# Squares from SBUF, other kept pieces and a rearranged tail in the normalisation stage of a four-layer image kernel

## The chip, the cores and the metric

The kernel runs on one core of one Trainium2 chip, as one launch. The metric is the device time of that launch in microseconds (us). The core has a matrix engine (TensorE, PE in the profile; PEld is its weight load), a vector engine (VectorE, DVE), an activation engine (ScalarE, ACT), a general engine (GpSimd, POOL) and a synchronising engine (SyncE, SP) that mostly issues transfers. Matrix products land in PSUM[...]; everything else lies in SBUF (128 partitions) or in DRAM.

## What is computed

The input `x` is an image of 256 x 256 pixels with 128 channels, float32. Four layers follow each other; each normalises its input over groups of four channels and adds its result to it. Only the first layer's beginning is touched by the change:

```python
# layer 0: attention over each image row, 4 heads of 32 channels
z   = _gn(x)                                   # group normalisation over the whole image
mu  = mean(z, axis=-1);  var = mean((z - mu)**2, axis=-1)
zn  = (z - mu) * rsqrt(var + 1e-5) * ln_scale + ln_bias
q, k, v, g = zn @ Wq, zn @ Wk, zn @ Wv, sigmoid(zn @ Wg)
bias = zn @ Wb                                 # one number per pixel and head
a = softmax(q k^T / sqrt(32) + bias)           # per image row and head; the bias is shared by all rows
x = x + (g * (a v)) @ Wo
```

The later layers (a gated recurrence of 16 steps, a triangle product and a 3 x 3 convolution) come after it and are the same in both kernels.

## The kernel before

The image has 65,536 pixels; they are worked in 32 pieces of 2048 pixels (1 MiB each), numbered m = 0 to 31.

**Statistics pass** (`statistics`, line 206). All 32 pieces are read once, for the mean and variance of each channel. Eight of them stay in SBUF (`kept`, line 360): pieces 0, 4, 8, ..., 28. The pass reads the other pieces first, the kept ones last. At its end `group_affine` and `centering` make a matrix `lc` and a column `cb`, so that `lc` times a piece, plus `cb`, is the group-normalised piece with its channel mean already taken away.

**Normalisation stage** (`attention`, lines 376 to 503), where the change lies. Pieces that were not kept are read again, three ahead, through SP's queue (`load`, buffers `xin`, three of them). A piece goes through these steps:

- `turn(m)`: sixteen 128 x 128 transposes on TensorE into two PSUM tiles `pt`, copied to `xo` (channels on partitions) by ACT (first half) and DVE (second half). Then the next piece's `load`, and POOL's queue stores `xo` to DRAM (`xT`), except for the last three pieces.
- `centre(m)`: for each half b, `zc = lc x xo` on TensorE, into a PSUM tile of 1024 columns. Then ACT squares `zc + cb` into `sq`, and DVE adds `cb` to `zc` and writes `zn`. Both read the same PSUM tile.
- `variance(m)`: TensorE takes the mean of the squares over the channels (`var`, four parts side by side on 32 partitions each); ACT makes `rs = exp(-0.5 ln(var + eps))`.
- `normalise(m)`: TensorE spreads `rs` over the partitions (`pr`, four products of 32 rows each, two per half, two instructions each); DVE multiplies `zn` by it, half by half; POOL applies `ln_scale` and `ln_bias` and its queue stores `zn` to DRAM (`znT`), except for the last three pieces.
- `pair_bias(m)`: TensorE makes the bias of the piece's pixels (`pbias`), DVE copies it (`bi`), and four small stores of 8 KB put it into DRAM (`biasD`) through SP's queue.

The order is written out by hand: nearly all instructions of this stage are pinned to program order on their engine (`mm`, `act`, `tt`, `ts`, `copy`, `transpose`, `acopy`); only transfers, and POOL's scaling, are placed by the framework's planner. The loop of one pass m is

```python
variance(m); centre(m + 1); normalise(m); pair_bias(m - 1); turn(m + 2)
```

The PSUM tiles of `zc`, `pr` and `pt` share one pool of three buffers ("w"[...]), taken in turn; `var`, `pbias` and the projections' `pp...` share a pool of two ("r"). A product can start only when all readers of the tile that last used its buffer are done.

**The tail.** The last three pieces stay in SBUF for the attention loop. Before it starts, `project(n, names)` makes q, k, v and g of the first three row pairs (n = 0, 1, 2) from piece 29: one product each, and a copy by ACT (g through an exponential). `project(0, ...)` stands in the last pass between `centre` and `normalise`; the others after the loop. `load_bias(r0, r1)` brings rows of the bias back from DRAM; the last 16 rows need the bias stores of pieces 30 and 31. After them TensorE transposes the bias (`pbt`, line 745), DVE copies it (`bT`), and the attention loop can add it to its first scores.

The printed code below has `attention`, with all these steps, at the line numbers of the profile.

Of the kernel before, what the change touches and what calls it, by code (L numbers as in the profile page):

```python
# [9 lines left out]
F32 = mybir.dt.float32  # L10
AF = mybir.ActivationFunctionType
# [6 lines left out]
P = 128  # L18
# [3 lines left out]
NH, HD = 4, 32  # L22
# [9 lines left out]
class Kernel:  # L32
# [21 lines left out]
    def act(self, out, in_, func, bias=0.0, scale=1.0, **kw):  # L54
        return self.nc.scalar.activation(out, in_, func, bias=bias, scale=scale, **kw)  # L55
# [4 lines left out]
    def mm(self, out, lhsT, rhs, start=True, stop=True):  # L60
        return self.nc.tensor.matmul(out, lhsT, rhs, start=start, stop=stop)  # L61
# [286 lines left out]
    def attention(self, wp, later, xT, x1T, znT, biasD, HD_, stats1, shift1):  # L348
        nc, tc, I = self.nc, self.tc, self.i
        V = nc.vector  # L350
        x = I["x"].rearrange("b h w c -> (b h w) c")
        NM = NPIX // 2048
        src = lambda m: x[m * 2048:(m + 1) * 2048].rearrange("(b p t) c -> p b (t c)", b=2, t=8)
        with ExitStack() as c:

            bias = wp.tile([P, 2, NH, N], F32, name="bias")
            c1 = c.enter_context(ExitStack())
            kp = c1.enter_context(self.pool(name="kp", bufs=1))

            kept = {m: kp.tile([P, 2, 1024], F32, name=f"kept{m}") for m in range(0, 32, 4)}  # L360
            mv, (w, (lns, lnb), wo, small) = self.statistics(wp, self.attention_weights(wp), HD_, kept, src)
            with self.pool(name="awq", bufs=2, space=PSUM) as ps0:
                ab, mg, _ = self.group_affine(wp, ps0, None, self.g4, "0", True, mv=mv)
                V.tensor_scalar_mul(shift1, mg, -1.0)
                lc, cb = self.centering(wp, ps0, ab, "0")

            def load_bias(r0, r1):
                rows = biasD.rearrange("h (j k) -> j h k", k=N)
                while r0 < r1:
                    t = min(r1, (r0 // P + 1) * P)  # L370
                    nc.sync.dma_start(bias[r0 % P:r0 % P + t - r0, r0 // P], rows[r0:t])
                    r0 = t
# [16 lines left out]
            mm, act, tt, ts, copy = pin(self.mm), pin(self.act), pin(V.tensor_tensor), pin(V.tensor_scalar_add), pin(V.tensor_copy)  # L389
            transpose, acopy = pin(nc.tensor.transpose), pin(nc.scalar.copy)  # L390
            xin, xo, zn, sq, rs = dict(kept), {}, {}, {}, {}
# [11 lines left out]
            def turn(m):  # L403
                if m >= NM:
                    return
                xo[m] = zp.tile([P, 2, P, 8], F32, name="xo")
                for b in range(2):
                    pt = wide("pt").rearrange("c (t p) -> c t p", t=8)
                    for t in range(8):
                        transpose(pt[:, t], xin[m][:, b, t * P:(t + 1) * P], self.ident)  # L410
                    (copy if b else acopy)(xo[m][:, b], pt.rearrange("c t p -> c p t"))
                if m not in kept:
                    load()
                if m < NM - HELD:
                    nc.gpsimd.dma_start(xT[:, m * 2048:(m + 1) * 2048], xo[m].rearrange("c b p t -> c (b p t)"))

            def centre(m):
                if m >= NM:
                    return
                zn[m] = yp.tile([P, 2048], F32, name="zn")  # L420
                for b in range(2):
                    zc = wide("zc")
                    for k in range(2):
                        mm(zc[:, k * 512:(k + 1) * 512], lc, xo[m][:, b].rearrange("c p t -> c (p t)")[:, k * 512:(k + 1) * 512])
                    sq[m, b] = work.tile([P, 1024], F32, name="sq")
                    act(sq[m, b], zc, AF.Square, bias=cb)
                    ts(zn[m][:, b * 1024:(b + 1) * 1024], zc, cb)

            def variance(m):
                var = row("var")  # L430
                for k in range(4):
                    mm(var[32 * k:32 * k + 32], m32, sq[m, k // 2][:, (k % 2) * 512:(k % 2 + 1) * 512])
                rs[m] = work.tile([P, 512], F32, name="rs")
                act(rs[m], var, AF.Ln, bias=self.eps)
                act(rs[m], rs[m], AF.Exp, scale=-0.5)

            def normalise(m):
                pr = [wide("pr") for _ in range(2)]
                for k in range(4):
                    mm(pr[k // 2][:, (k % 2) * 512:(k % 2 + 1) * 512], spread[32 * k:32 * k + 32], rs[m][32 * k:32 * k + 32])  # L440
                for b in range(2):
                    z = zn[m][:, b * 1024:(b + 1) * 1024]
                    tt(z, z, pr[b], ALU.mult)
                    nc.gpsimd.tensor_scalar(z, z, lns, lnb, ALU.mult, ALU.add)
                if m < NM - HELD:
                    nc.gpsimd.dma_start(znT[:, m * 2048:(m + 1) * 2048], zn[m])

            def pair_bias(m):
                if m < 0:
                    return  # L450
                pb = row("pbias")
                for k in range(4):
                    mm(pb[32 * k:32 * k + 32], w["32"], zn[m][:, k * 512:(k + 1) * 512])
                bi = io.tile([P, 512], F32, name="bi")
                copy(bi, pb)
                for k in range(4):
                    s = m * 2048 + k * 512
                    nc.sync.dma_start(biasD[:, s:s + 512], bi[32 * k:32 * k + NH])

            tc.keep_in_program_order(self.table(LN_EXP))  # L460
            for _ in range(3):
# [1 line left out]
            turn(0)  # L463
            turn(1)
            centre(0)
            early = {}

            def project(n, names):
                if n not in early:
                    early[n] = qp.tile([P, 4, 512], F32, name="proj", tag="xin")  # L470
                z = zn[NM - HELD][:, n * 512:(n + 1) * 512]
                for nm in names:
                    pp, o = row("pp" + nm), early[n][:, "qkvg".index(nm)]
                    if nm == "v":
                        for ch in range(4):
                            mm(pp[:, ch * P:(ch + 1) * P], z[:, ch * P:(ch + 1) * P], w["v"])
                    else:
                        mm(pp, w[nm], z)
                    if nm == "g":
                        act(o, pp, AF.Exp, scale=-1.0)  # L480
                    else:
                        act(o, pp, AF.Identity)

            for m in range(NM):
                variance(m)
                centre(m + 1)
                if m == NM - 1:
                    project(0, "qkvg")
                normalise(m)
                pair_bias(m - 1)  # L490
                turn(m + 2)
                if m == 5:
                    self.later_weights(later)
                elif m == 12:
                    self.first_rows = self.row_transforms(later.tile([P, 2, HC], F32, name="hs0"), HD_, 0)
                elif m == NM - 4:
                    load_bias(0, 192)
                elif m == NM - 1:
                    load_bias(192, 240)
            project(1, "qkvg")  # L500
            pair_bias(NM - 1)
            load_bias(240, 256)
            project(2, "qkvg")
            c1.close()
            held = {m: (zn[m], xo[m].rearrange("c b p t -> c (b p t)")) for m in range(NM - HELD, NM)}
# [1135 lines left out]
```

## Time and profile before

| | us |
|---|---|
| median of 3 runs | 4903.11 (4900.88 to 4903.68) |
| the profiled execution: time | 4899.83 |
| the profiled execution: span | 4897.9 |
| TensorE busy | 4716.3 (96%) |
| VectorE busy | 3631.1 (74%) |
| ScalarE busy | 3334.3 (68%) |
| GpSimd busy | 1855.8 (38%) |
| normalisation stage, first `turn` to the bias transposes | 131.8 to 462.0 |

In a row of the timeline, the first two numbers are the start and the length in us; then come the engine, the line of the code that issued it (a helper's line for most: 61 is `mm`, 55 is `act`, 388 is the pinning lambda), the operation, output <- inputs, and the tile shapes. In brackets stands how long the engine had been idle just before, and what ended that. In a row of the chain, there are the start, the length, engine, tile and count. A matrix product in float32 is two instructions, so "x8" means four products. Columns of the windows are explained where they are shown. The PE clock is the share of full speed that TensorE was granted.

### The profile page before, as it was taken

How to read it: one execution, taken by the hardware profiler on the slowest of the kernel's cores; microseconds unless marked ns; L12 is line 12 of the kernel's file. 1: busy time of each engine (PE TensorE's matmuls, PEld its weight loads, DVE VectorE, ACT ScalarE, POOL GpSimd, SP SyncE). 2: the span in 40 equal slices, each digit the busy share in tenths (PEclk: the TensorE clock that was granted, in tenths of full speed). 3: DMA queues.
4: the chain of work that ended last, by engine and by line, in shares of the span. 5: the costliest groups of instructions: out<-in, count | busy, mean ns of one | idle time of the engine just before them, and what ended most of it. 6: DMA issues, size and time to landing. Idle time of an engine off the chain costs nothing.

```text
span 4897.9 us, 78226 instructions
## 1 busy us (share of the span) xinstructions
PE 4716.3 (96%) x30415; PEld 2682.4 (55%) x30415; DVE 3631.1 (74%) x4551; ACT 3334.3 (68%) x5009; POOL 1855.8 (38%) x1290
## 2 busy tenths in 40 slices
PE   8999999999999899999999997999999999999999
PEld 2444555555555433333333332269999943369999
DVE  6666777777777699999999996763533357789886
ACT  6445888888888799999999995543333367762110
POOL 0233555555555466666666664421011000000000
PEclk9999999999999999999999998999999999999999
DMA  8784122222222245555555555986766688854432
GB/s 299 278 315 161 42 85 80 86 83 87 83 87 83 77 101 132 131 132 132 136 131 131 133 132 133 333 328 226 280 243 225 223 336 323 328 206 166 141 123 70
DMA packets 221057, 835.13 MB, mean 171 GB/s; under 512 B 59046, under 2 KB 62396, under 8 KB 172148
## 3 DMA queue, kind: packets, MB, share of 16 engines
q1 hardware_dynamic: 144638, 498.23, 29.7%
q0 software_dynamic: 74752, 331.47, 23.3%
q8 instruction: 244, 4.00, 0.3%
q14 instruction: 127, 1.04, 0.1%
q10 hardware_dynamic: 1296, 0.40, 0.0%
HBM read 497.84 MB, written 265.03 MB: 156 GB/s over the span
## 4 chain that ended last, share of the span: by engine, by line
PE 66%; ACT 14%; DVE 11%; issue 5%; DMA 2%; POOL 1%; SPq 1%; ACTq 0%; DVEq 0%; POOLq 0%
PE z L61 9%; PE m L61 8%; PE zc L61 7%; PE nd L61 7%; PE sc L61 6%; PE po L61 5%; PE ppq L61 3%; PE ppv L61 3%; PE pe L61 2%; PE px L61 2%; PE ppk L61 2%; PE ppg L61 2%; PE py L61 2%; PE pr L61 2%; ACT L946 2%
## 5 line engine op out<-in xcount | busy, mean ns | idle before, releaser
L605 DVE TENSOR_TENSOR e<-sc,bT 128x1024 f32<-128x1024 f32 x512 | 613.7, 1220 | 254.8 <-PE sc L61 254.8
L605 POOL TENSOR_TENSOR ks<-e 128x1024 f32<-128x1024 f32 x256 | 602.1, 2371 | 445.5 <-PE nd L61 428.4
L55 ACT ACTIVATE e<-e 128x1024 f32<-128x1024 f32 x512 | 539.4, 1054 | 41.2 <-DVE e L605 31.5
L1132 DVE TENSOR_TENSOR LR<-z,sg 128x512 f32<-128x512 f32 x256 | 268.5, 1049 | 363.0 <-ACT sg L55 363.0
L61 PE MATMUL m<-U,v 128*128 128x128 f32 x4608 | 514.8, 275 | 0.0
L61 PEld LDWEIGHTS m<-U,v 128*128 128x128 f32 x4608 | 514.6, 192 | 0.0
L61 PE MATMUL z<-wf,zt 128*128 128x128 f32 x4096 | 459.6, 276 | 1.4 <-DVE zn L1132 1.4
L61 PEld LDWEIGHTS z<-wf,zt 128*128 128x128 f32 x4096 | 459.4, 193 | 2.4 <-DVE zn L1132 2.2
L55 ACT ACTIVATE sg<-z 128x512 f32<-128x512 f32 x256 | 152.8, 597 | 307.8 <-PE z L61 307.8
L1264 POOL DMA_DIRECT2D prodD<-o x128 | 69.0, 540 | 617.4 <-ACT o L55 607.5
L61 PE MATMUL sc<-proj 32*128 32x256 f32 x4096 | 299.8, 403 | 3.2 <-DVE e L605 2.4
L974 POOL TENSOR_TENSOR fs<-f 128x512 f32<-128x512 f32 x64 | 177.0, 2766 | 279.3 <-DVE f L971 258.7
L61 PEld LDWEIGHTS sc<-proj 32*128 32x128 f32 x4096 | 188.1, 185 | 160.7 <-PE px L61 94.8
L61 PE MATMUL nd<-e,proj 128*32 128x256 f32 x4096 | 272.8, 384 | 2.6 <-DVE og L605 2.6
L55 ACT ACTIVATE dn<-dn 128x512 f32<-128x512 f32 x384 | 238.0, 620 | 11.1 <-DVE dn L605 7.0
L974 POOL TENSOR_TENSOR u<-t,tr 128x512 f32<-128x512 f32 x64 | 229.7, 3589 | 9.8 <-DVE tr L977 8.4
L974 POOL TENSOR_TENSOR t<-t,v 128x1024 f32<-128x1024 f32 x64 | 209.5, 3274 | 53.5 <-DVE t L971 53.5
L61 PE MATMUL po<-LR 128*128 128x256 f32 x1024 | 222.1, 379 | 6.9 <-DVE LR L1132 6.9
L1517 ACT COPY m4s<-m 128x512 f32<-128x512 f32 x32 | 18.6, 583 | 287.3 <-PE m L61 287.3
L61 PEld LDWEIGHTS po<-LR 128*128 128x128 f32 x1024 | 194.3, 190 | 33.9 <-DVE LR L1132 7.7
L1527 POOL DMA_DIRECT2D out_dram<-ys x32 | 37.0, 1155 | 423.9 <-DVE ys L1525 423.9
L61 PE MATMUL av<-y,ident 128*128 128x512 f32 x384 | 192.4, 610 | 4.0 <-DVE y L971 4.0
(380 smaller groups left out, 10696.7 us busy)
## 6 DMA issues: line engine op xcount, KB each, us to landing
zt<-znT SPq DMA_DIRECT2D x128, 1024.0 KB
xin<-x2T SPq DMA_DIRECT2D x64, 1024.0 KB
znT<-zn POOLq DMA_DIRECT2D x61, 1024.0 KB, 5.2
xin<-in_x_dram SPq DMA_DIRECT2D x48, 1024.0 KB
xr<-x3T SPq DMA_DIRECT2D x46, 768.0 KB
x1T<-x POOLq DMA_DIRECT2D x64, 512.0 KB, 4.9
xf<-x1T SPq DMA_DIRECT2D x64, 512.0 KB
xc<-x1T SPq DMA_DIRECT2D x128, 256.0 KB
```

What stands on the lines that cost most here:

```text
L55: return self.nc.scalar.activation(out, in_, func, bias=bias, scale=scale, **kw)
L61: return self.nc.tensor.matmul(out, lhsT, rhs, start=start, stop=stop)
L605: pin = lambda f: lambda *a, **k: tc.keep_in_program_order(f(*a, **k))
L946: pin(nc.scalar.preload_act_table_set(want))
L974: pin(nc.gpsimd.tensor_tensor(out, a, b_, op))
L1132: pin = lambda f: lambda *a, **k: tc.keep_in_program_order(f(*a, **k))
L1264: nc.gpsimd.dma_start(prodD[g * CQ + d].rearrange("(p a j) -> p a j", p=P, a=2), o.rearrange("p a j b -> p a (j b)"))
L1517: nc.scalar.copy(m4, m[4])
L1527: nc.gpsimd.dma_start(out[row:row + 8].rearrange("r p t c -> p (r t) c"), ys.rearrange("p g k t c -> p (g k t) c"))
```

## The change

Four edits, all in `attention`:

1. In `centre`, DVE's add comes first and writes `zn`; ACT then squares the half from `zn` in SBUF, without a bias, in place of `zc + cb` from PSUM.
2. The kept pieces are 0, 1, 2, 7, 12, 17, 22 and 26 in place of every fourth.
3. The four bias stores of each of the last two pieces alternate between SP's and POOL's queue.
4. Of `project(0)`, only q and k stay ahead of the last `normalise`; v and g come after the loop. Of `project(1)`, only q stays ahead of the last `pair_bias` and `load_bias`; k, v and g come after them.

```diff
-            kept = {m: kp.tile([P, 2, 1024], F32, name=f"kept{m}") for m in range(0, 32, 4)}
+            kept = {m: kp.tile([P, 2, 1024], F32, name=f"kept{m}") for m in (0, 1, 2, 7, 12, 17, 22, 26)}
...
                     sq[m, b] = work.tile([P, 1024], F32, name="sq")
-                    act(sq[m, b], zc, AF.Square, bias=cb)
-                    ts(zn[m][:, b * 1024:(b + 1) * 1024], zc, cb)
+                    z = zn[m][:, b * 1024:(b + 1) * 1024]
+                    ts(z, zc, cb)
+                    act(sq[m, b], z, AF.Square)
...
                 for k in range(4):
                     s = m * 2048 + k * 512
-                    nc.sync.dma_start(biasD[:, s:s + 512], bi[32 * k:32 * k + NH])
+                    q = (nc.sync, nc.gpsimd)[k % 2] if m >= NM - 2 else nc.sync
+                    q.dma_start(biasD[:, s:s + 512], bi[32 * k:32 * k + NH])
...
                 centre(m + 1)
                 if m == NM - 1:
-                    project(0, "qkvg")
+                    project(0, "qk")
                 normalise(m)
...
-            project(1, "qkvg")
+            project(0, "vg")
+            project(1, "q")
             pair_bias(NM - 1)
             load_bias(240, 256)
+            project(1, "kvg")
             project(2, "qkvg")
             c1.close()
```

## The prediction

> **What bounds the kernel now.** I read the page first: TensorE is busy 96% of the span. The change touches one stage, between the statistics pass (ends near 126 us) and the attention loop (from about 462 us), so I went there with the chain that ended last, windows and the timeline. The chain, cut to two passes of the loop over m:
>
> ```profile
> 306.54 1.00 PE pbias L61 x8
> 307.53 1.90 PE pt L388 x16
> 309.43 1.00 PE var L61 x8
> 310.42 3.63 PE zc L61 x8
> 314.05 1.99 PE pr L61 x8
> 316.05 1.00 PE pbias L61 x8
> ```
>
> One pass takes 9.51 us (314.05 less 304.54), and only TensorE is on the chain. The window says the same, and what else is loaded (columns: start:end, length, busy of PE, PEld, DVE, ACT, POOL, PE clock, DMA share, GB/s):
>
> ```profile
> 200.00:300.00 100.00, 100.00 (x516) 43.28 (x520) 70.11 (x65) 47.66 (x52) 36.09 (x42) 1.00 0.85 312
> 326.30:335.80 9.50, 9.50 (x52) 4.08 (x48) 6.55 (x7) 4.57 (x5) 3.49 (x4) 1.00 0.94 385
> 136.00:140.00 4.00, 0.15 (x1) 0.18 (x2) 0.00 (x0) 0.00 (x0) 0.21 (x1) 0.51 0.90 310
> ```
>
> But busy is not working at its peak. `pr` is eight matmuls on 32 rows each: 1.99 us here, 1.07 us (446.86 to 447.93) in the last pass. The timeline says why:
>
> ```profile
> 302.86 1.11 ACT L55 ACTIVATE sq<-zc,cb 128x1024 f32<-128x1024 f32 x1 [0.54 <-PE zc L61]
> 304.07 1.28 DVE L388 TENSOR_SCALAR zn<-zc,cb 128x1024 f32<-128x1024 f32 x1 [2.58 <-issue]
> 304.47 0.30 PEld L61 LDWEIGHTS pr<-rs,spread 32*128 32x128 f32 x4 [0.76 <-ACT sq L55]
> 305.41 0.30 PEld L61 LDWEIGHTS pr<-rs,spread 32*128 32x128 f32 x4 [0.64 <-DVE zn L388]
> ...
> 446.86 1.14 PE L61 MATMUL pr<-rs,spread 32*128 32x512 f32 x8
> ```
>
> The square of the first half reads `zc` from 302.86 to 303.97, the add reads the same buffer from 304.07 to 305.35, and at 305.41 the second four weight loads of `pr` start: they need that buffer (three PSUM buffers serve zc, zc, pr, pr, pt, pt in turn). In the last pass the buffers are long free and the eight run together. DVE had been idle 2.58 us before 304.07.
>
> Two places at the ends:
>
> ```profile
> 139.85 3.44 PE L388 MATMUL pt<-ident,xin 128*128 128x128 f32 x16 [6.05 <-DMA xin<-in_x_dram]
> 443.10 1.12 PE L61 MATMUL ppq<-zn,wq 128*128 128x512 f32 x2 [1.54 <-DVE bi L388]
> 451.04 1.12 PE L61 MATMUL ppk<-zn,rawk 128*128 128x512 f32 x2 [0.99 <-DVE bi L388]
> 460.26 1.75 PE L745 MATMUL pbt<-ident,bias 128*128 128x128 f32 x14 [1.31 <-DMA bias<-biasD]
> ```
>
> **What the Trainium skill says.** *PSUM — Partial Sum Buffer*, "PSUM bank collisions raise a hardware error": two engines on one bank and quadrant must be kept apart, reads against reads included. The trace agrees: every add starts 0.03 to 0.10 us after its square ends. *TensorEngine Tiling (Array Packing)*, "Key Properties": different tiles can load weights and multiply in parallel; here 1.07 against 1.99 us. *TensorE: Matmul & The Clock Gate*, "Part 1: The HAM clock gate": an idle TensorE is put to half clock and needs some 3.4 us of work to return. Here 0.51 at 136 to 140 us, and those transposes take 3.2 us where the ones before took 1.9.
>
> **Part 1: add first, square from SBUF.** Removed: the square's read of `zc`. The add (1.28 us) now starts when `zc` is ready, the square after it. A square from SBUF is 1.054 us in the statistics pass (`sqx`), 1.113 here: 0.06 x 64, on ACT, idle half the time, so worth nothing. Following one pass on the old clock:
> - add b0: 302.9 to 304.2, before `pr` begins (304.47). So all eight `pr` run together: 304.47 to 305.54.
> - `pbias` to 306.54; `pt` needs the buffer of `zc` b1: add b1 304.55 to 305.85, free. Its second half needs `pr` b0: multiply 305.85 to 307.02, transposes there at 307.5. `pt` ends 308.44.
> - square b0 304.3 to 305.35, b1 305.9 to 306.95; `var` needs both at 308.44: 1.5 us spare. `var` to 309.43.
> - DVE: second multiply to 308.2, `bi` copy to 308.9, `xo` copy to 310.1; wanted by `zc` b1 at 311.2. ACT's `xo` copy 307.7 to 308.7, wanted at 309.43.
> Nothing else is late, so the pass becomes, of the chain's rows, 1.00+1.90+1.00+3.63+1.07 = 8.60 us, 0.92 less. DVE (6.55 us), ACT (4.57) and POOL (3.49) still fit.
>
> The transfers have to follow. Two of 1.049 MB are stored per pass and one loaded in four passes of five: 14.7 MB in 43.0 us, 341 GB/s. Before: 11.5 MB in 38.0, 303; the window of 100 us shows 312 at a share of 0.85, so 367 GB/s at full share, and single windows have 385. It fits, at about 0.93. A load has three passes of lead, a store two to three; `xT` lands in 9.9 us (median). Cost taken: nothing; bound: 0 to +0.4 us a pass.
>
> **Part 2: pieces 0, 1, 2 kept.** Piece 1's second load, issued at 134.43, held TensorE from 133.8 to 139.85 and put its clock down. Now `pt(1)` follows at 133.8 and ends at 135.75; `zc(0)` starts there in place of 143.13: 7.4 us. Part 1 gives some back: `var(0)` now waits for add and square in series. zc(0) ends 139.4, add b1 139.5 to 140.8, square to 141.9, `var` to 142.9 against 148.91. `zc(1)` to 146.55, add b1 to 148.0, which frees `pt(2)`: 148.05 against 155.14. **Gain 7.1 us.** The first new wait could be for piece 3: its load goes out at 134.4, and it is transposed at about 157. The bytes of all passes are the same as before.
>
> **Loop.** From `pt(2)` to `pt(31)` there are 29 passes, `pr` in each: 29 x 0.92 = **26.7 us**. The `zc` of piece 31 then ends near 404, against 437.65.
>
> **Part 3: the tail.** From the end of zc(31) to the last transposes of the bias, before: 437.65 to 460.26 = 22.6 us. After, as offsets:
> - `pr` 1.07, `pbias(29)` 2.07. `var(31)` waits for its second square (2.45): ends 3.5.
> - `ppq(0)` needs the buffer of `pbias(29)`: DVE does add, two multiplies, copy until 4.4. `ppq`, `ppk` end 6.3, `pr(31)` 7.35, `pbias(30)` 8.35, `ppv` 9.3.
> - `ppg(0)` needs the buffer of `pbias(30)`, whose copy waits behind the multiplies of piece 31 (7.5 to 9.85) until 10.55: a new stall of about 1.3 us. `ppg` ends 11.5, `ppq(1)` 12.4.
> - `pbias(31)` 12.5 to 13.5 (POOL finished piece 31 at 11.1); then seven projections of 0.93 cover its way to DRAM and back, to 20.0.
> - That way: copy to 14.35, then as before from 455.73 to 460.26, 4.5 us: 18.9. With two of four stores on POOL's queue it is between 0.7 shorter (two SP issues of 0.35 less) and 0.7 longer: *DMA: Bandwidth & Descriptors*, "Anatomy of one DMA", puts the fixed cost of a POOL-issued transfer at about 2 us, no such small one is in the trace. Either is inside 20.0. Were that cover gone it would cost up to 0.7. POOL has nothing else due: the next fold is at 467.9 us before.
> The transposes, now all 16, start at 20.0; two of them (0.24) had been done early. So **2.3 us**, 0.9 of it the `pr` of pass 30.
>
> **Sum.** 7.1 + 26.7 + 2.3 = 36.1 us. Span 4897.9 to 4861.8; the profiled execution took 4899.83, 1.93 more than its span, so 4863.7. The median is 3.28 above that: 4903.11 - 36.1 = **4867 us**. The attention loop and all later stages keep their code; I take them as shifted. Its first matmuls run at half clock (0.50 from 468 to 476 us) after the tail's waits; fewer waits may spare some of this, or not: 0 to -4 us, or +2 where the clock's windows fall worse elsewhere.
>
> **Rivals.**
> - *The transfers become the bound.* For: 0.93 needed, four heavy passes in a row (366 GB/s), windows of a pass before show shares of 0.91 at only 328. Against: three passes of lead, and 429 GB/s from 148 to 152 us. At 326 GB/s a pass takes 9.0 us: 29 x 0.4 = 12 back, 4879.
> - *The release is early but `pr` stays at two and two* (multiplies or a semaphore hold the second pair). For: in the loop it has never been seen together. Against: the 1.07 in the last pass. Then only the ends: 7.1 + 1.4, 4895.
> - *A wait in place of the one removed, slower.* The square now stands behind the add, and `var` behind both. If it came over 1.5 us later than worked out, `var` would hold TensorE; to lose 9.8 us in all, with 8.5 from the ends, a pass must grow by 0.63, so the second square must be 1.5 + 0.92 + 0.63 = 3.0 us late. Only `multiply` x2 ahead of the second add would do that, and the order is written out. From there about 4915.
> - *The planner orders unpinned transfers otherwise*, a load behind bias stores: a pass or two held, +3 to +10: inside the range, and counted in the forecast's own.
>
> **How the numbers follow.** As forecast 0.72 (own range 4861 to 4876); transfers 0.13; no overlap 0.09; slower 0.04; elsewhere 0.02. A measurement can tell about 0.2%, 9.8 us. The range 4860 to 4885 leaves out the last three cases (0.15) and some 0.04 of the first, where the clock spares more than 4 us. Faster: the first two and two thirds of the third, 0.91; same: its other third and "elsewhere", 0.05; slower 0.04.
>
> **What would show it.** `pr` x8 at about 1.07 in every pass; passes of 8.6 us; adds starting before squares, idle before `pr` on DVE's add gone; no wait for `xin` at 139 and clock 1.00 there; no wait of `pbt` for `bias`, a wait of `ppg` for `bi` of 1.3 us. Wrong if `pt` waits for `xin` in the loop, `zc` for `xo`, `var` for `sq`, or if the attention loop's own passes change.

## The result and the profile after

| | before, us | after, us |
|---|---|---|
| median of 4 runs | 4902.92 (4900.88 to 4903.68) | 4862.09 (4859.07 to 4863.21) |
| profiled execution: time | 4899.83 | 4863.21 |
| profiled execution: span | 4897.9 | 4861.1 |

The ratio is 0.9916, with a 95% interval of 0.9899 to 0.9934: 41 us less, between 32 and 50. (A fourth run of the kernel before has joined the three of the table above.) The profiled executions are 36.6 us apart; the forecast was 36.1, which with its 4867 lies inside that interval. The medians are 4 us further apart than the profiled pair. Of the kernel before, the profiled execution was faster than all four runs of the table; of the kernel after, it was the slowest of the four. What the traces explain below is the 36.6 us of this pair.

The chain that ended last, of the changed kernel, over two passes of the loop (start, length, engine, tile, count):

```profile
302.91 1.07 PE pr L61 x8
303.98 1.00 PE pbias L61 x8
304.97 1.90 PE pt L388 x16
306.87 0.99 PE var L61 x8
307.87 3.63 PE zc L61 x8
311.50 1.07 PE pr L61 x8
```

The pass is 8.59 us (311.50 less 302.91). Four of its five parts have the lengths they had; `pr` alone went from 1.99 to 1.07. The timeline of the same pass shows the new order of the two readers (it has `pr` 0.07 us earlier than the chain):

```profile
301.29 1.28 DVE L388 TENSOR_SCALAR zn<-zc,cb 128x1024 f32<-128x1024 f32 x1 [1.66 <-issue]
302.61 1.06 ACT L55 ACTIVATE sq<-zn 128x1024 f32<-128x1024 f32 x1 [1.91 <-DVE zn L388]
302.84 0.31 PEld L61 LDWEIGHTS pr<-rs,spread 32*128 32x128 f32 x8 [0.76 <-issue]
302.84 1.14 PE L61 MATMUL pr<-rs,spread 32*128 32x512 f32 x8
304.27 1.06 ACT L55 ACTIVATE sq<-zn 128x1024 f32<-128x1024 f32 x1 [0.60 <-DVE zn L388]
306.80 0.16 PEld L61 LDWEIGHTS var<-sq,mean 128*32 128x32 f32 x8 [0.17 <-issue]
```

The add is done at 302.57, before `pr` begins at 302.84, so all eight weight loads stand in one row and none waits for DVE. The second square ends at 305.33; `var` starts at 306.80 and had 1.47 us to spare.

The windows (start:end, length, busy of PE, PEld, DVE, ACT, POOL, PE clock, DMA share, GB/s):

```profile
136.00:140.00 4.00, 3.77 (x20) 2.39 (x19) 2.48 (x3) 1.08 (x2) 1.12 (x2) 1.00 0.62 197
200.00:300.00 100.00, 100.00 (x570) 44.33 (x567) 77.27 (x71) 52.23 (x59) 41.16 (x47) 1.00 0.91 338
```

TensorE's clock is at 1.00 where it had fallen to 0.51, and the transfers run at 338 GB/s and a share of 0.91.

The two ends, in the timeline:

```profile
133.89 3.68 PE L388 MATMUL pt<-ident,kept 128*128 128x128 f32 x32 [0.30 <-issue]
...
416.39 1.13 PE L61 MATMUL ppg<-zn,rawg 128*128 128x512 f32 x2 [1.03 <-DVE bi L388]
...
425.70 1.91 PE L749 MATMUL pbt<-ident,bias 128*128 128x128 f32 x16
```

The first two pieces are transposed in one go. The transposes of the bias follow the last projection with no wait; in its place `ppg(0)` waits for the copy `bi`.

To compare kernels whose statistics pass ended at different times, I use one distance from here on, "the stage": from the first `pt` to the first copy `bT`. Before it was 131.86 to 461.18, 329.3 us; after, 133.89 to 426.77, 292.9 us: 36.4 us less, all of the difference of the spans but 0.4. The 0.4 is what two larger differences leave, both outside the change: the first `pt` is 2.0 us later in the run after, and what follows `bT` 2.4 us shorter.

### The profile page after: what moved, and what is told of

It is laid out like the page before. It is cut to its first block, busy times and chain, and to the rows that moved or that the text cites. A ratio compares the mean times of both kernels' runs of the same rounds, so it can differ in the third digit from the quotient of the medians.

```text
span 4861.1 us, 78233 instructions
## 1 busy us (share of the span) xinstructions
PE 4680.3 (96%) x30415; PEld 2669.2 (55%) x30415; DVE 3632.2 (75%) x4551; ACT 3331.2 (69%) x5009; POOL 1858.4 (38%) x1294
## 4 chain that ended last, share of the span: by engine, by line
PE 66%; ACT 14%; DVE 11%; issue 6%; DMA 2%; POOL 1%; SPq 0%; ACTq 0%; DVEq 0%; POOLq 0%
PE z L61 9%; PE m L61 8%; PE zc L61 7%; PE nd L61 7%; PE sc L61 6%; PE po L61 5%; PE ppq L61 3%; PE ppv L61 3%; PE pe L61 2%; PE ppg L61 2%; PE ppk L61 2%; PE px L61 2%; PE py L61 2%; PE var L61 2%; ACT L950 2%
```

## Experiments

### Each part alone

**The first edit alone.**

```diff
-                    act(sq[m, b], zc, AF.Square, bias=cb)
-                    ts(zn[m][:, b * 1024:(b + 1) * 1024], zc, cb)
+                    z = zn[m][:, b * 1024:(b + 1) * 1024]
+                    ts(z, zc, cb)
+                    act(sq[m, b], z, AF.Square)
```

> The kernel before with only the first edit: DVE adds first, ACT squares the half from SBUF. My theory (the early release of the zc buffer lets all eight pr instructions run together): a pass of 8.60 us in place of 9.51, pr at 1.07 in place of 1.99; 29 passes give 26.7 us, the last pr 0.9, the start neither gives nor takes more than 0.3 us. In all 27 to 28.5 us less: about 4875. If pr did not run together in the loop: a pass of 9.5 us and 4900 to 4903.

Measured: 4875.15 us, ratio 0.9942 (0.9925 to 0.9958); the stage 302.0 us, 27.3 less. Its chain:

```profile
308.29 1.07 PE pr L61 x8
309.36 1.00 PE pbias L61 x8
310.35 1.90 PE pt L388 x16
312.25 0.99 PE var L61 x8
313.25 3.63 PE zc L61 x8
316.88 1.07 PE pr L61 x8
```

The pass of 8.59 us is there with this edit alone. The edit does not touch the tail, and the bias transposes still wait (1.76 us at 433.29).

**The second edit alone.**

```diff
-            kept = {m: kp.tile([P, 2, 1024], F32, name=f"kept{m}") for m in range(0, 32, 4)}
+            kept = {m: kp.tile([P, 2, 1024], F32, name=f"kept{m}") for m in (0, 1, 2, 7, 12, 17, 22, 26)}
```

> The kernel before with only the second edit, the kept pieces 0, 1, 2, 7, 12, 17, 22, 26. My theory: the wait of the second piece's transposes for xin (6.05 us) and their half clock go, 7.4 us less, about 4895.5, with passes of 9.51 us as before. Rival, the transfers are hidden anyway or the stall only moves to piece 3: no change, 4902 to 4904, and a wait for xin of several us at piece 3.

Measured: 4898.1 us, ratio 0.9989 (0.9982 to 0.9996), that is 2 to 9 us less; the stage 322.0 us, 7.3 less. `pt(0)` and `pt(1)` stand in one row:

```profile
133.66 3.68 PE L388 MATMUL pt<-ident,kept 128*128 128x128 f32 x32 [0.30 <-issue]
```

The clock from 134 to 138 us is 1.00, and the pass is 9.51 us as before. In its list of waits from 125 to 200 us nothing waits for `xin`: the stall went, it did not move to piece 3.

**The third and fourth edits alone** (stores of the last two pieces on two queues, projections rearranged).

> The kernel before with only the third and fourth edits (bias stores of the last two pieces on two queues; v, g of project(0) and k, v, g of project(1) later). My theory: the bias transposes no longer wait for the bias (1.31 us), ppg(0) waits about 1 us for bi instead; 1.4 us less from the end of zc(31) to the first bT copy (23.5 us before), which the times can hardly tell: 4901 to 4902.5. Rival, the stores on the other queue land later and the wait stays: 4903 to 4904.

Measured: ratio 0.9998 (0.9989 to 1.0007), which tells nothing; the trace does: the stage is 327.3 us, 2.0 less. Its timeline:

```profile
443.04 1.12 PE L61 MATMUL ppq<-zn,wq 128*128 128x512 f32 x2 [1.54 <-DVE bi L388]
...
449.13 1.12 PE L61 MATMUL ppg<-zn,rawg 128*128 128x512 f32 x2 [0.96 <-DVE bi L388]
...
458.44 1.91 PE L748 MATMUL pbt<-ident,bias 128*128 128x128 f32 x16
```

The wait of `pbt` is gone, and so is that of `ppk(1)` (0.99 before); `ppg(0)` waits 0.96. From the end of `zc(31)` to the first `bT` it takes 21.9 us, 1.6 less than before, against 1.4 expected. The other 0.4 of the 2.0 lie at the start of the stage, which these edits do not touch: the wait for `xin` was 5.56 us in this run and 6.05 before.

The three stages add up: 27.3 + 7.3 + 2.0 = 36.6, and the whole change has 36.4. So the parts neither help nor hinder one another by more than some tenths, and a difference of less than half a microsecond between two stages can't be put down to an edit from one trace of each.

### Is it the last reader, or the earlier add?

The order of the two readers turned round, but the square still reads PSUM:

```diff
-                    act(sq[m, b], zc, AF.Square, bias=cb)
-                    ts(zn[m][:, b * 1024:(b + 1) * 1024], zc, cb)
+                    z = zn[m][:, b * 1024:(b + 1) * 1024]
+                    ts(z, zc, cb)
+                    act(sq[m, b], zc, AF.Square, bias=cb)
```

> The kernel before with the order of the two readers turned round but the square still reading zc from PSUM with its bias: DVE adds first, ACT squares zc + cb after it. My theory (what counts is when the last reader of the PSUM buffer is done): the buffer of half 0 is free at the same time as before, pr stays at two and two, a pass of 9.4 to 9.6 us, 4900 to 4906. Rival, that DVE simply starts earlier is what helps, or the multiply behind it: a pass near 8.6 us and 4875.

Measured: 4903.09 us, ratio 1.0000 (0.9991 to 1.0008); the stage 329.5 us. Its timeline:

```profile
306.49 1.28 DVE L388 TENSOR_SCALAR zn<-zc,cb 128x1024 f32<-128x1024 f32 x1 [1.69 <-PE zc L61]
307.81 1.11 ACT L55 ACTIVATE sq<-zc,cb 128x1024 f32<-128x1024 f32 x1 [1.92 <-DVE zn L388]
308.04 0.30 PEld L61 LDWEIGHTS pr<-rs,spread 32*128 32x128 f32 x4 [0.76 <-issue]
308.97 0.30 PEld L61 LDWEIGHTS pr<-rs,spread 32*128 32x128 f32 x4 [0.64 <-ACT sq L55]
```

DVE adds as early as in the changed kernel, and nothing is gained: the second four loads of `pr` wait for the square, until 308.92, in place of the add. So the gain of the first edit is the release of the PSUM buffer by its last reader, and the square's new source is what makes the release early.

### How near the transfers are

**Every piece read again.** Pieces 7, 12, 17, 22 and 26 are kept in the statistics pass but read again in the stage:

```diff
-            xin, xo, zn, sq, rs = dict(kept), {}, {}, {}, {}
+            xin, xo, zn, sq, rs = {m: kept[m] for m in (0, 1, 2)}, {}, {}, {}, {}
...
-            again = [m for m in range(NM) if m not in kept]
+            again = list(range(3, NM))
...
-                if m not in kept:
+                if m > 2:
                     load()
```

> The changed kernel, but pieces 7, 12, 17, 22 and 26, though kept in the statistics pass, are read again like the others: three transfers of 1.049 MB in every pass, 366 GB/s at 8.59 us. Theory: TensorE bounds the pass and the transfers only follow; the changed kernel moved 338 GB/s at a share of 0.91, so 371 at full share, and this just fits: a pass of 8.6 to 8.7 us, 4862 to 4866. Rival (the transfers are already the bound of the changed kernel, or within a hair): a pass of 9.0 us or more and 4874 or more, with waits for xin or for the store of xo.

**A fourth transfer a pass.**

```diff
                     nc.gpsimd.dma_start(xT[:, m * 2048:(m + 1) * 2048], xo[m].rearrange("c b p t -> c (b p t)"))
+                    nc.gpsimd.dma_start(x1T[:, m * 2048:(m + 1) * 2048], xo[m].rearrange("c b p t -> c (b p t)"))
```

> The changed kernel with a fourth transfer in each pass, a second store of xo into a buffer of DRAM that is overwritten later: 19 MiB in five passes, 463 GB/s at 8.59 us, more than can be moved. It measures where the transfers take over. Theory, a ceiling of 371 GB/s: a pass of 10.7 us, about 55 us more in 26 passes, 4917. If the ceiling is the 429 GB/s of the best window: 9.3 us and 4880. If transfers cost nothing whatever their number: 4862.

Measured, with all read again: 4859.45 us, ratio 0.9917 (0.9901 to 0.9934), the stage 292.9 us, the same. With the fourth transfer: 4912.7 us, ratio 1.0021 (1.0011 to 1.0031), the stage 340.2 us, 47.4 more than in the changed kernel. One window of each, first all read again, then the fourth transfer:

```profile
300.00:380.00 80.00, 80.00 (x451) 34.66 (x449) 61.34 (x57) 41.78 (x47) 31.36 (x36) 1.00 1.01 380
```

```profile
200.00:300.00 100.00, 93.20 (x461) 41.15 (x458) 62.71 (x58) 41.89 (x48) 38.46 (x47) 0.93 0.98 397
```

With three transfers a pass TensorE is still busy all the time; with four it is not, and its clock falls too. Now DVE's add waits for the store that still reads its `zn` buffer; from the list of waits:

```profile
DVE zn L388 <- DMA znT<-zn: 51.0, 12, 5.8
```

(us in total, times, the longest.) Over one stretch for all, 160 to 380 us, the changed kernel moved 345 GB/s, the one with all read again 372 at no cost, and the one with the fourth transfer 395, held back by its stores. So the limit for such transfers lies above 372 and, over a long stretch, at about 395; the changed kernel is 13% under that. The fourth transfer goes through POOL's queue like the other stores; whether this queue or all transfers together set the limit, no run tells apart, though the share of 0.98 speaks for the latter. Pieces 7, 12, 17, 22 and 26 need not be kept for the time of this stage; that pieces 0, 1 and 2 are kept is worth the 7.3 us of the second edit.

### How much room the square has

Every square of the changed kernel made two and three times over:

```diff
-                    act(sq[m, b], z, AF.Square)
+                    for _ in range(2):
+                        act(sq[m, b], z, AF.Square)
```

(This is the first of two kernels; the second has range(3).)

> The changed kernel with every square of the stage made twice, to measure the room that is left behind the add: 1.06 us more per half on ACT. Theory: var has about 1.5 us to spare after the second square (305.33 against 306.80 in the changed kernel); the second squares now end at 306.85, ACT's copy of xo at 307.9 in place of 307.05, wanted at 307.80: a pass of 8.6 to 8.9 us, 4862 to 4871. Rival, that ACT's chain is already on the edge: a pass longer by most of the 2.1 us, 4900 or more.

> The same with every square made three times: the room is used up, the last square ends 2.1 us after var wants it, and ACT's copy of xo 2.25 us after zc wants it: a pass of about 10.8 us, 65 us more in 29 passes, 4927. If nothing waits for the square: 4862.

Measured, twice: 4867.53 us (ratio 0.9932, 0.9909 to 0.9954), a pass of 8.62 us, the stage 297.8. Three times: 4935.68 us (1.0072, 1.0049 to 1.0095), a pass of 10.79 us (one `pr` starts at 303.97, the next at 314.76), the stage 367.4, and `var` now waits for the square in every pass:

```profile
310.15 1.05 PE L61 MATMUL var<-sq,mean 128*32 128x512 f32 x4 [1.17 <-ACT sq L55]
```

The start of the stage, where nothing hides the square, pays at once: from the first `pt` to `pt(2)` 16.1 us in the changed kernel, 19.1 with two squares, 21.4 with three; with the 0.9 us in the loop that explains most of the 4.9 us that two squares cost. In the loop, 2.1 us more on ACT were free and 4.2 cost 2.2. This agrees with the room of 1.5 us seen in the trace: ACT was idle for 0.60 us between the two squares of a pass, so 2.1 us more work moves the end of the last one by only 1.5, and the room is just used up.

### The stores on two queues

The third edit undone in the changed kernel:

```diff
-                    q = (nc.sync, nc.gpsimd)[k % 2] if m >= NM - 2 else nc.sync
-                    q.dma_start(biasD[:, s:s + 512], bi[32 * k:32 * k + NH])
+                    nc.sync.dma_start(biasD[:, s:s + 512], bi[32 * k:32 * k + NH])
```

> The changed kernel with its third edit undone: all bias stores on SP's queue. Theory: the seven projections cover the way of the bias in either case, so the distance from the end of zc(31) to the first bT copy stays at 20.8 to 20.9 us and the time at 4862; the load of the last bias rows goes out about 0.6 us earlier after the copy of bi (2.5 us, 3.1 with POOL's queue). Rival, that the split of the stores is what ended the wait for the bias: the distance grows by 0.5 us or more and the bias transposes wait again.

Measured: 4863.34 us, ratio 0.9922 (0.9905 to 0.9938); the stage 292.9 us, the same. From the end of the copy `bi` (418.69) to the issue of the last load (421.66) it is 2.97 us; with the two queues 420.13 to 423.23, 3.10. POOL issued its second store by 421.42, and the load could go 1.8 us later; the page *DMA: Bandwidth & Descriptors* of the Trainium skill puts the fixed cost of such a transfer ("Anatomy of one DMA") at about 2 us, and this agrees. So in the changed kernel the third edit brings nothing and costs 0.1 us that is hidden; I had expected it to cost 0.6. The gain of the tail is the fourth edit's. What the third edit would do without the fourth, where the bias is waited for, was not run.

### A version to beat both

This starts from the kernel of the last experiment, with all bias stores on SP's queue. It adds three things: the bias of piece 30 before the last `normalise`, k of `project(1)` before the last bias, and products without use (`filler`) between the first scores, to keep TensorE busy.

```diff
                 if m == NM - 1:
                     project(0, "qk")
+                    pair_bias(m - 1)
                 normalise(m)
-                pair_bias(m - 1)
+                if m < NM - 1:
+                    pair_bias(m - 1)
...
-            project(1, "q")
+            project(1, "qk")
             pair_bias(NM - 1)
             load_bias(240, 256)
-            project(1, "kvg")
+            project(1, "vg")
...
+            def filler(n):
+                f = ps.tile([P, P], F32, name="filler", tag="nd0", bufs=1)
+                for _ in range(n):
+                    mm(f, self.ident, self.cmat)
+
+            filler(2)
             for i in range(2):
                 score(i)
+                filler(4 + 2 * i)
```

> A version to beat both: the changed kernel with all bias stores on SP, the bias of piece 30 made before the normalisation of piece 31 (so that ppg(0) no longer waits 1.03 us for bi behind the two multiplies), k of project(1) ahead of the bias of piece 31, and 2, 4 and 6 products without use between the bias transposes and the third score, to keep TensorE's clock up (it was 0.50 from 433 to 445 us). Theory: 0.5 to 1.0 us less up to the first bT copy (20.85 after the end of zc(31) before), and, if the clock stays at full speed, 2 to 4 us less to the second nd group (26.3 us after the first bT copy in the changed kernel): about 4858. Rival, the useless products only delay the scores or the clock falls all the same: 4861 to 4864.

Measured: 4864.59 us, ratio 0.9925 (0.9908 to 0.9941), not to be told from the changed kernel. In the trace the first half works: the wait of `ppg(0)` is gone and the stage is 292.1 us, 0.8 less. The second half can't be told. The clock is at full speed until 436 us (0.57 in the next 4 us), and from the first `bT` to the `nd` of the second pass (TensorE's products of the exponentials with v) it takes 24.2 us in place of 26.2. But the eleven other kernels, which have the same instructions there and no filler, take 24.9 to 26.6, so at most 0.7 us lies outside what varies by itself. And the attention loop (layer 0's loop over row pairs, whose output tile is `x1`) gives most of the 2.0 us back at its end: the last two stores of `x1` are 14.55 us apart, against 13.00 in the changed kernel. In this run the clock falls there:

```profile
1642.00:1646.00 4.00, 3.74 (x29) 1.49 (x19) 1.06 (x3) 0.85 (x2) 0.00 (x0) 0.66 0.00 0
```

It falls there in the kernel before too (14.67 us), and not in the changed kernel. From the first `pt` to the last store of `x1` it is 1517.3 us against 1518.4.

## Why the prediction was right

The mechanism it named is the one that the runs show, and the sizes of its parts came within half a microsecond each. Point by point, in the order of its parts:

- **Part 1**, the mechanism and the size: `pr` at 1.07, a pass of 8.59 against 8.60. The turned order without the new source shows that it is the buffer's last reader, and the first edit alone shows the pass. Of the clock times worked out for one pass, the add before `pr`, the square's end (1.5 us spare, 1.47 seen) and DVE's order all came so.
- **Transfers**: a share of 0.93 and 341 GB/s were worked out, 0.91 and 338 came. The rival of the transfers was given 9.0 us a pass at 326 GB/s; 372 went without any cost. The step that took 367 GB/s for the most that can be moved was wrong. It scaled 312 GB/s at a share of 0.85 up to a share of 1.00, and the share did grow so (0.91 at 338, 1.00 at 372), but 1.00 was not the limit: with the fourth transfer 395 went at 0.98.
- **Part 2**: 23.3 us from the first `pt` to `pt(2)` before, 133.89 to 150.03 = 16.1 after: 7.1, as forecast. (One reading was off, without use in the sum: the transposes at half clock took 3.44 us; the 3.2 is the time of their weight loads.) Part 1 was to give back some 0.3 us here (7.4 to 7.1), as the square now stands in series with the add; it was 0.1, for with the second edit alone this stretch takes 16.0 us.
- **Loop**: 155.14 to 437.65 before, 150.03 to 405.92 after: 26.6 us against 26.7.
- **Tail**: from the end of `zc(31)` to the first `bT`, 437.65 to 461.18 = 23.5 before and 405.92 to 426.77 = 20.85 after: 2.7 against 2.3 forecast. The stall of `ppg(0)`, forecast at 1.3, was 1.03, and the wait of `ppq(0)` was 0.72, where 0.9 was implied (3.5 to 4.4). The cover of the bias held. The third edit was left open between 0.7 gained and 0.7 lost, inside the cover; it turned out to be worth nothing.
- **Shifted rest**: from `bT` to the end, 4436.7 and 4434.3 us. The forecast gave the clock 0 to -4 us here. The start of the attention loop did not gain by fewer waits: the clock was at 0.50 from 434 to 442 us, somewhat longer than before, and the second pass's `nd` came 26.2 us after `bT` in place of 24.9. The end of the loop took 1.7 us less (13.00 in place of 14.67), so the loop as a whole is 0.5 us shorter; the other 1.8 us lie in later layers, and their cause is open.
- **Sum**: the profiled execution was forecast at 4863.7 us and took 4863.21. This is closer than the method is: the later first `pt` (+2.0), which nobody foresaw, and the shorter rest (-2.4), which was left out of the sum, happen to cancel, and that is luck. The median was forecast at 4867, by putting the 3.28 us between profiled execution and median of the kernel before on top; of the kernel after, the median lies 1.1 us below the profiled execution, so this step failed: the forecast is 5 us above the median, about as much as the runs of one kernel scatter.

Of the rivals, the transfers were shut out by the run with all pieces read again, "two and two" by the `pr` rows (in the loop no weight load of `pr` waits for DVE or ACT any more), and the wait in place of the one removed by the repeated squares: 2.1 us more on ACT cost 0.03 us a pass, and only with 4.2 us more does `var` hold TensorE.

## What to carry to other kernels

A matrix engine that reads 100% busy may still have a stretch that could be shorter: compare the same group of products where its buffers are free and where they are not. A PSUM buffer is free when its last reader is done, so where two engines read it one after the other, let the second read the copy that the first writes to SBUF. This pays if the copy is made anyway and the second engine has time to spare; merely changing the order of the two readers gained nothing here. Ask of each queue move whether the thing behind it was waited for at all: here the reordered projections hid the way of the bias, and the second queue had nothing left to shorten.

## What was not expected

- The attention loop has the same instructions after `bT` in eleven of the twelve kernels (the twelfth has the filler), and yet its beginning and its end differ from run to run. From `bT` to the second pass's `nd` it takes 24.2 to 26.6 us, and between the last two stores of `x1` either 13.0 us (nine runs) or 14.5 to 14.7 (before, the second edit alone, the filler). These three are the ones with the shortest beginnings, 24.2 to 24.9 us. From `bT` to the last store all twelve lie between 1224.7 and 1226.2 us: what is won at the one end is mostly lost at the other. That this comes from when the clock falls is my reading; no run tests it. It is enough to hide a gain of 1 or 2 us elsewhere.
- The clock fell to 0.50 at the start of the attention loop though TensorE was busy 3.13 and 2.83 of the 4 us from 426 and 430 us, with no gap over 0.93 us between its products, and it stayed there while TensorE was busy 3.50 of 4.
- The first `pt` came between 131.6 and 134.6 us in the twelve profiled runs, whose statistics passes have equally many instructions of each kind; where the kernels differ by 1 to 2 us, the span cannot tell it and a distance inside the stage can.
- One core moved 397 GB/s over 100 us with loads and stores mixed, 30 more than the 367 that I had drawn from the share.
